# A GNN layer with a mixture of experts on one core: 18 of 49 result tiles gathered inside the edge loop

## The chip, the core and the metric

The kernel runs on one core of a Trainium2 chip. A core has a matrix engine (PE, with PEld for its weight loads), a vector engine (DVE), a scalar engine (ACT), GpSimd (POOL) and a sync engine (SP). Each takes its instructions in the order in which the program issued them. SP, ACT and POOL also issue DMAs, and a DMA that has to wait for a buffer or for another engine's result holds up everything behind it in the same queue. Times are device microseconds of one launch; lower is better.

## The reference

There are 6250 nodes with 256 features in float32 and 100000 edges, sorted by their target node. The layer is a graph step followed by a feed-forward step with experts:

```
xh  = layernorm(x)
agg = segment_sum(xh[src], dst) / max(degree, 1)
x1  = x + concat(xh, agg) @ W.T + b
xn  = layernorm(layernorm(x1)) * gamma + beta
logits = xn @ Wr + br;  two best of 8 experts, softmax over those two
out = x1 + sum over the two experts of  w_e * (gelu(xn @ W1[e] + b1[e]) @ W2[e] + b2[e])
```

Each expert has 512 hidden units. Every node thus needs its own row x1 and two rows of expert results, which lie at places that only the routing knows.

## The kernel before

**Tiles.** The 100000 edges are padded to 784 edge tiles of 128 edges: 56 windows (`W`) of 14 tiles (`C`). A window of edges belongs to at most 128 neighbouring nodes. Four windows form a chunk (14 chunks, `K`); chunks form three batches of 8, 5 and 1 chunks. For the output, the nodes are cut once more into 49 node tiles of 128 rows (the last has 106).

**Start.** The kernel multiplies all node rows by the neighbour half of W and writes the product to the DRAM tensor `z_d`; the own half goes to `u_d` a little later, in tasks that run beside the first edge tiles.

**Edge loop.** Tile `t` is handled as follows. POOL has earlier issued an indirect DMA (`gather`, line 601) that fetches 128 rows of `z_d` into buffer `xg[t % XG]`; there are `XG` = 28 such buffers, and the loop issues the gather of tile t + XG right behind the matmul of tile t, because that matmul frees the buffer. PE multiplies the buffer by a one-hot matrix that DVE built (`hot_tiles`, line 612) and adds it to the window's sum in PSUM (`add_edges`, line 618). One-hots are built half a window at a time, about half a window ahead. When a window is complete, DVE divides by the degree and adds u (`window_x1`, lines 658 to 660), and SP writes the new node rows to `x1_d` (line 661), at a row that is only known at run time. When a chunk is complete, routing follows: norms, logits, ranks, counts, one-hot matrices for sorting tokens by expert (lines 697 and 705), and a plan that is written to DRAM and read back by node tile (`plans`).

**Order by hand.** The order on all engines is written out. `at(t, f)` puts a step behind edge tile t. `after(t)` runs those steps, then expert tasks at a given pace (each task has a cost in us, and a tile allows 0.72, 0.6 in the last 56 tiles, more behind the loop), then `sum_rows`. The expert tasks of a chunk (`expert_stages`: 8 experts in pairs, lines 884, 889, 897, 901, 903) start 60 tiles behind the chunk's end, fewer for the last chunks. A batch also has a few tiles of overflow rows (`more_stages`, lines 927 to 952), which come behind its last chunk. Expert results go to the DRAM tensor `y_d`.

**The sums.** `start_experts` appends the chunk's node tiles to the list `sums`. For a node tile, `gather_rows` has SP load the 128 rows of x1 (line 973) and POOL gather two sets of 128 rows from `y_d` (line 976), into three buffers that `spare()` hands out from the ring of `xg` buffers. `add_rows` has DVE do two multiply-adds (line 983) and SP write the output (line 985). `sum_rows` issues them: it waits until the batch of the node tile has issued all its results (`batch.left` is 0) and until fewer than XG edge tiles are left, as the ring then has buffers that no edge tile needs any more:

```
while sums and not sums[0][0].batch.left and clock >= due and left < XG:
    if 0 < left < XG and spares + 3 > XG - left:
        return
```

The adds are kept in a list `adds`. One is issued when more than XG // 3 - 1 (8) node tiles wait in it or, behind the loop, when the planner's clock has come to `added`, which advances by 2.5 per node tile. Node tiles 0 to 26 belong to batch 0, 27 to 44 to batch 1, 45 to 48 to batch 2.

A branch at the end (lines 1171 to 1261) computes the same without these assumptions on the order of edges; it isn't taken here.

Of the kernel before, what the change touches and what calls it, by code (L numbers as in the profile page):

```python
# [8 lines left out]
F32 = mybir.dt.float32  # L9
# [8 lines left out]
P = 128  # L18
EPS = 1e-5
C = 14  # L20
# [4 lines left out]
BATCHES = (8, 8), (5, 5), (1, 2)  # L25
GB = 3
LATE = 40
XG = 28
RAW = 1
LATE_CHUNKS = 4  # L30

# [2 lines left out]
def gnn_ffn_kernel(ctx: ExitStack, tc: tile.TileContext, x, x_cols, src, dst, dst_next, gw, gw_t, gb, gb_cols, gamma, beta,  # L34
# [36 lines left out]
    N, D = x.shape  # L71
# [5 lines left out]
    W = src.shape[1]  # L77
# [49 lines left out]
    edges = fast_pools.enter_context(tc.tile_pool(name="edges", bufs=1))  # L127
# [6 lines left out]
    early = early_pools.enter_context(tc.tile_pool(name="early", bufs=2, side="right"))  # L134
# [31 lines left out]
    dst_i = const.tile([P, W, C], I32, name="dst_i")  # L166
    xg = [edges.tile([P, DA], F32, name=f"xg{i}") for i in range(XG)]

# [431 lines left out]
    def gather(g, c):  # L600
        nc.gpsimd.indirect_dma_start(  # L601
            out=xg[(g * C + c) % XG][:, :DZ], out_offset=None, in_=z_d[:, :],
            in_offset=bass.IndirectOffsetOnAxis(ap=src_i[:, g, c:c + 1], axis=0))
# [11 lines left out]
    def add_edges(V, c):  # L615
        if c == 0:
            V.pS = ps.tile([P, DA], F32, name="pS")
        nc.tensor.matmul(V.pS, V.hot[c // HC][:, c % HC, :], xg[(V.g * C + c) % XG],  # L618
                         start=(c == 0), stop=(c == C - 1))
# [342 lines left out]
    def spare():  # L962

        nonlocal spares
        spares += 1
        return xg[(W * C + spares - 1) % XG][:, :D]


    def gather_rows(K, n, V):
        V.rows = slice(n * P, min((n + 1) * P, N))  # L970
        count = V.rows.stop - V.rows.start
        V.o = spare()[:count]
        nc.sync.dma_start(V.o, x1_d[V.rows, :])
        V.y2 = [spare()[:count] for _ in range(2)]
        for r in range(2):
            nc.gpsimd.indirect_dma_start(  # L976
                out=V.y2[r], out_offset=None, in_=y_d[:K.batch.end_row, :],
                in_offset=bass.IndirectOffsetOnAxis(ap=plans[:count, n, r:r + 1], axis=0))

    def add_rows(n, V):  # L980
        count = V.rows.stop - V.rows.start
        for r in range(2):
            nc.vector.scalar_tensor_tensor(V.o, V.y2[r], plans.bitcast(F32)[:count, n, 2 + r:3 + r], V.o,  # L983
                                           op0=ALU.mult, op1=ALU.add)
        nc.sync.dma_start(out[V.rows, :], V.o)
# [3 lines left out]

    tasks, later, Ks, sums, adds = [], {}, [], [], []  # L990
    slots, w1_sb, w2_sb, xe = None, None, None, None
    now, spent, clock, due, added, spares = None, 0.0, 0.0, 0.0, 0.0, 0
    class Steps:

        x1, var, roots, norms, route, exps, weigh, choices, count = 2, 5, 7, 9, 11, 14, 15, 16, 19
# [15 lines left out]
    def at(t, f, *args):  # L1011
        later.setdefault(max(t, now), []).append(lambda: f(*args))
# [51 lines left out]
    def sum_rows():  # L1064

        nonlocal due, added
        if now < W * C:
            added = clock + 3.0
        while adds and now >= W * C and (added <= clock or not (sums or tasks)):
            adds.pop(0)()  # L1070
            added += 2.5
        left = W * C - 1 - now
        while sums and not sums[0][0].batch.left and clock >= due and left < XG:
            if 0 < left < XG and spares + 3 > XG - left:
                return
            K, n = sums.pop(0)
            V = Group()
            gather_rows(K, n, V)
            adds.append(lambda n=n, V=V: add_rows(n, V))
            while len(adds) > XG // 3 - 1:  # L1080
                adds.pop(0)()
                added += 2.5
            due = max(due, clock - 6.0) + (4.0 if left > 0 else 2.4)

    def after(t):
        nonlocal now, spent, clock
        now = t
        while later.get(t):
            later[t].pop(0)()
        later.pop(t, None)  # L1090
        clock += 0.6 if t < W * C else 0.3 if tasks else 1.2

        pace = 0.6 if W * C - 56 <= t < W * C else 0.72 if t < W * C else 1.2 if len(Ks) < W // CW else 2.0
        spent = min(spent + pace, pace) if tasks else 0.0
        while tasks and spent > 0:
            us, f, _ = tasks.pop(0)
            spent -= us
            clock += us
            f()
        sum_rows()  # L1100

    def new_window(g, V_before):
        V = Group()
        V.g, V.before, V.hot = g, V_before, []
        hot_tiles(V, 0)
        return V

    now = 0
    V = new_window(0, None)
# [6 lines left out]
    for index in range(W // CW):  # L1116
        K = Group()
# [9 lines left out]
        for g in range(K.first, K.first + CW):  # L1127
            if g > 0:
                V = V_next
# [41 lines left out]
    with tc.If(wrong_r > 0), tc.tile_pool(name="gp", bufs=1) as gp:  # L1171
# [9 lines left out]
        with tc.For_i(0, W * C) as j:  # L1181
# [18 lines left out]

            spare = gp.tile([P, 1], F32, name="spare")
            nc.vector.scalar_tensor_tensor(spare, lane, float(N), own, op0=ALU.add, op1=ALU.subtract)
            nc.vector.scalar_tensor_tensor(spare, count, 0.0, spare, op0=ALU.is_gt, op1=ALU.mult)
            to = gp.tile([P, 1], I32, name="to")
# [107 lines left out]
```

## Time and profile before

| what | value |
|---|---|
| time, median of 17 runs | 1197.09 us (1192.41 to 1202.67) |
| profiled execution: time | 1196.68 us |
| profiled execution: span | 1194.9 us, mean granted clock of PE 0.949 |
| PE busy | 1058.1 us (89%) |
| POOL busy | 845.4 us (71%) |
| DVE busy | 688.1 us (58%) |
| ACT busy | 463.3 us (39%) |
| software DMA queue (POOL's gathers) | 118.91 MB, 40.3% of 16 engines' span |
| first and last edge gather on POOL | 75.5 and 1046.0 us |
| first and last gather of expert rows on POOL | 1047.2 and 1182.5 us |

How to read the profile's rows: a group is "line engine operation output<-input xcount | busy us, mean ns of one | idle us of that engine just before, and what ended it". A row of the timeline is "start us, duration us, engine, line, operation, count, and in brackets the idle time before it and its releaser". A row of waits is "who <- for whom: total us, times, longest us". "issue" as releaser means that nothing in the profile was waited for. A row of a table by stretch is "from:to, length, busy us (count) for each engine, granted clock, DMA share, GB/s".

### The profile page before, as it was taken

The numbers are of one execution on the slowest core, as the hardware profiler recorded it, in microseconds if no ns is written. First come the engines' busy times: TensorE is split into PE (matmuls) and PEld (weight loads), VectorE is DVE, ScalarE is ACT, GpSimd is POOL, SyncE is SP. The second block draws the span as 40 slices with busy tenths as digits, with TensorE's granted clock in tenths as the row PEclk, the third lists the DMA queues.
The fourth block names the chain that finished last, engine by engine and source line by source line (L and its number), as shares of the span: only waits on it lengthen the run. The fifth ranks groups of instructions, "written<-read, shape, count | busy, mean of one in ns | idle before, by whom it ended". The sixth has DMA issues, their size and how long they took to land. (4 is left out here: it accounts for less than half of the span.)

```text
span 1194.9 us, 18881 instructions
## 1 busy us (share of the span) xinstructions
PE 1058.1 (89%) x5352; PEld 860.8 (72%) x5352; DVE 688.1 (58%) x2433; ACT 463.3 (39%) x1281; POOL 845.4 (71%) x892
## 2 busy tenths in 40 slices
PE   7939977899989999898999979899999999988970
PEld 6828755688858778586877858578888887875750
DVE  5757878565735555364655536465572745557642
ACT  2430001635334534443453444434552543642510
POOL 0077677777777777777777777777777777777574
PEclk9969997999989999898998989999999999997995
DMA  9978989656564564656465465554656564676784
GB/s 330 357 236 267 318 283 314 128 141 146 144 145 132 147 142 136 133 143 140 136 148 142 136 132 143 135 148 137 141 138 154 144 155 131 139 225 194 202 244 131
DMA packets 143578, 210.08 MB, mean 176 GB/s; under 512 B 36652, under 2 KB 111128, under 8 KB 143340
## 3 DMA queue, kind: packets, MB, share of 16 engines
q0 software_dynamic: 42768, 118.91, 40.3%
q1 hardware_dynamic: 92364, 80.45, 21.2%
q10 hardware_dynamic: 8336, 9.45, 2.4%
q8 instruction: 45, 0.74, 0.3%
q14 instruction: 65, 0.53, 0.1%
HBM read 163.86 MB, written 44.86 MB: 175 GB/s over the span
## 5 line engine op out<-in xcount | busy, mean ns | idle before, releaser
L601 POOL DMA_INDIRECT xg<-z_d,src_i x770 | 732.8, 952 | 237.7 <-issue 105.4
L618 PE MATMUL pS<-xg,hot 128*128 128x265 f32 x1568 | 436.1, 402 | 52.9 <-DMA xg<-z_d,src_i 28.8
L618 PEld LDWEIGHTS pS<-xg,hot 128*128 128x128 f32 x1568 | 287.0, 194 | 134.0 <-DMA xg<-z_d,src_i 49.0
L884 PEld LDWEIGHTS ph<-xe,w_sb 128*128 128x128 f32 x1792 | 224.9, 199 | 15.1 <-ACT xe L859 6.2
L884 PE MATMUL ph<-xe,w_sb 128*128 128x128 f32 x1792 | 227.4, 283 | 4.8 <-ACT xe L859 4.8
L897 PE MATMUL py<-w_sb,hid 128*128 128x256 f32 x896 | 216.4, 386 | 1.8 <-DVE rows L901 1.8
L612 DVE TENSOR_TENSOR hot<-cols,rel 128x896 f32<-128x896 f32 x112 | 121.6, 1087 | 136.6 <-PE pS L618 134.1
L889 ACT ACTIVATE hid<-ph,b_sb 128x128 f32<-128x128 f32 x448 | 127.5, 368 | 179.3 <-PE ph L884 179.0
L897 PEld LDWEIGHTS py<-w_sb,hid 128*128 128x128 f32 x896 | 170.3, 192 | 33.8 <-issue 6.8
L859 ACT ACTIVATE xe<-xs x448 | 139.3, 311 | 86.2 <-ACT xe L859 36.4
L976 POOL DMA_INDIRECT xg<-y_d,plans x98 | 96.9, 989 | 40.2 <-issue 16.2
L708 ACT ACTIVATE xs<-pm,beta_sb,gamma_sb 128x256 f32<-128x256 f32 x112 | 57.1, 560 | 133.4 <-PE pm L705 133.0
L901 DVE TENSOR_TENSOR rows<-py,b_sb 128x512 f32<-128x512 f32 x56 | 38.5, 687 | 116.2 <-PE py L897 116.1
L640 ACT ACTIVATE sums<-pS 128x265 f32<-128x265 f32 x55 | 21.3, 388 | 111.2 <-PE pS L618 108.0
L271 PE MATMUL ph<-gc,x_t 128*128 128x264 f32 (+1 forms) x200 | 57.9, 415 | 7.2 <-ACT zt L295 5.7
L705 PE MATMUL pm<-to,xn 128*128 128x256 f32 x224 | 59.0, 387 | 5.3 <-DVE to L698 5.3
L660 DVE SCALAR_TENSOR_TENSOR x<-pS,rdeg,x 128x264 f32<-128x264 f32 x55 | 27.1, 493 | 61.5 <-DMA x<-u_d 60.1
L983 DVE SCALAR_TENSOR_TENSOR xg<-xg,plans,xg 128x256 f32<-128x256 f32 (+1 forms) x98 | 45.8, 483 | 19.8 <-DMA xg<-y_d,plans 14.0
L330 POOL DMA_INDIRECT xg<-x_dram,src_i x14 | 13.4, 959 | 59.9 <-DMA src_i<-src_dram 56.0
L889 ACT ACT_TABLE_LOAD x25 | 32.1, 1283 | 55.8 <-PE ph L884 55.6
L271 PE MATMUL pm<-gc,x_t 128*128 128x264 f32 (+1 forms) x192 | 53.4, 402 | 0.0
L705 PEld LDWEIGHTS pm<-to,xn 128*128 128x128 f32 x224 | 43.2, 194 | 14.1 <-issue 4.7
(214 smaller groups left out, 889.9 us busy)
## 6 DMA issues: line engine op xcount, KB each, us to landing
y_d<-rows SPq DMA_DIRECT2D x56, 256.0 KB
xg<-z_d,src_i POOLq DMA_INDIRECT x770
w_sb<-w_dram ACTq DMA_DIRECT2D x16, 512.0 KB
x<-u_d SPq DMA_DIRECT2D x55, 132.0 KB
x_d<-x SPq DMA_DIRECT2D x55, 128.0 KB
u_d<-u_t SPq DMA_DIRECT2D x24, 264.0 KB
x_t<-x_cols_dram SPq DMA_DIRECT2D x12, 512.0 KB
xu<-x_dram SPq DMA_DIRECT2D x24, 256.0 KB
```

Of the source, the lines that this page charges most:

```text
L271: nc.tensor.matmul(pz, x_t[:, t, k, :], gc[:, h * KD + k, :n], start=(k == 0), stop=(k == KD - 1))
L601: nc.gpsimd.indirect_dma_start(out=xg[(g * C + c) % XG][:, :DZ], out_offset=None, in_=z_d[:, :], in_offset=bass.IndirectOffsetOnAxis(ap=sr ...
L612: nc.vector.tensor_tensor(hot, col[:, None, :].to_broadcast([P, HC, P]), V.rel[:, c:c + HC, None].to_broadcast([P, HC, P]), op=ALU.is_equal)
L618: nc.tensor.matmul(V.pS, V.hot[c // HC][:, c % HC, :], xg[(V.g * C + c) % XG], start=(c == 0), stop=(c == C - 1))
L705: nc.tensor.matmul(px[:, k, :], G.xn[i][:, k * P:(k + 1) * P], G.one_hot[i], start=True, stop=True)
L708: nc.scalar.activation(xs[:, at:at + 2 * P], px[:, k, :], AF.Identity, bias=beta_sb[:, k:k + 1], scale=gamma_sb[:, k:k + 1])
L859: nc.scalar.activation(xe[:, :, bass.ds(to_at, CAP)], src[:, :, bass.ds(src_at, CAP)], AF.Copy)
L884: nc.tensor.matmul(ph[:, i, a * SH:(a + 1) * SH], w1_sb[:, U.e + a, k, c * P:(c + 1) * P], xe[:, k, at:at + SH], start=(k == 0), stop=(k = ...
L889: nc.scalar.activation(U.hid[:, c, a * SH:(a + 1) * SH], ph[:, i, a * SH:(a + 1) * SH], AF.Gelu, bias=b1_sb[:, U.e + a, c:c + 1])
L897: nc.tensor.matmul(U.py[:, h, :], U.hid[:, c, h * P:(h + 1) * P], w2_sb[:, U.e + h, c, :], start=(c == 0), stop=(c == KH - 1))
L976: nc.gpsimd.indirect_dma_start(out=V.y2[r], out_offset=None, in_=y_d[:K.batch.end_row, :], in_offset=bass.IndirectOffsetOnAxis(ap=plans[:c ...
L983: nc.vector.scalar_tensor_tensor(V.o, V.y2[r], plans.bitcast(F32)[:count, n, 2 + r:3 + r], V.o, op0=ALU.mult, op1=ALU.add)
```

## The change

The number of edge buffers goes from 28 to 23, and six new buffers `yb` of 128 x 256 are added. From the moment batch 0 has issued its last result, and while more than 32 edge tiles are left, a node tile is gathered every 9 edge tiles, up to 18 of them. Such an early node tile uses three of the six `yb` buffers in turn, and its adds and its output write stand 8 edge tiles behind its gathers in the order. The other 31 node tiles are issued as before, when fewer than `XG` edge tiles (now 23) are left; their ring consists of the 23 edge buffers and the six new ones. The condition on `spares` in the last tiles of the loop, which keeps them off buffers that an edge tile still needs, now counts with 23.

```diff
-XG = 28
+XG = 23
+YB = 6
+EARLY, APART = 18, 9
...
-        return xg[(W * C + spares - 1) % XG][:, :D]
-    def gather_rows(K, n, V):
+        i = (spares - 1) % (XG + YB)
+        return xg[(W * C + i) % XG][:, :D] if i < XG else yb[i - XG]
+
+    yb = [edges.tile([P, D], F32, name=f"yb{i}") for i in range(YB)]
+
+    def early_sum():
+        nonlocal early, next_early
+        K, n = sums.pop(0)
+        V = Group()
+        kept = [yb[(3 * early + i) % YB] for i in range(3)]
+        gather_rows(K, n, V, lambda: kept.pop(0))
+        at(now + APART - 1, add_rows, n, V)
+        early += 1
+        next_early = now + APART
+
+    def gather_rows(K, n, V, spare):
...
         left = W * C - 1 - now
+        if sums and not sums[0][0].batch.left and early < EARLY and now >= next_early and left > XG + APART:
+            early_sum()
         while sums and not sums[0][0].batch.left and clock >= due and left < XG:
...
-            gather_rows(K, n, V)
+            gather_rows(K, n, V, spare)
             adds.append(lambda n=n, V=V: add_rows(n, V))
-            while len(adds) > XG // 3 - 1:
+            while len(adds) > (XG + YB) // 3 - 1:
```

With 29 buffers in the ring, the limit on node tiles waiting in `adds` stays at 8.

More of the change, by code (lines that the diff above doesn't have):

```diff
@@ L991, in gnn_ffn_kernel @@
     slots, w1_sb, w2_sb, xe = None, None, None, None
-    now, spent, clock, due, added, spares = None, 0.0, 0.0, 0.0, 0.0, 0
+    now, spent, clock, due, added, spares, early, next_early = None, 0.0, 0.0, 0.0, 0.0, 0, 0, 0
     class Steps:
```

## The prediction

> **What bounds the kernel now.** I read the page's groups first, then the waits of POOL, then the counts of edge matmuls and edge gathers side by side by stretches, and last the end of the trace queue by queue. From the page's groups:
> ```profile
> L601 POOL DMA_INDIRECT xg<-z_d,src_i x770 | 732.8, 952 | 237.7 <-issue 105.4
> L618 PE MATMUL pS<-xg,hot 128*128 128x265 f32 x1568 | 436.1, 402 | 52.9 <-DMA xg<-z_d,src_i 28.8
> L976 POOL DMA_INDIRECT xg<-y_d,plans x98 | 96.9, 989 | 40.2 <-issue 16.2
> L983 DVE SCALAR_TENSOR_TENSOR xg<-xg,plans,xg 128x256 f32<-128x256 f32 (+1 forms) x98 | 45.8, 483 | 19.8 <-DMA xg<-y_d,plans 14.0
> ```
> POOL looks 71% busy, with 238 us of idle time around its edge gathers. The timeline shows what that idle time is: in the loop and in the tail alike, one gather takes 0.95 us and the next begins 0.30 us later, whatever is named as releaser.
> ```profile
> 1043.47 0.95 POOL L601 DMA_INDIRECT xg<-z_d,src_i  x1 [0.30 <-PE pS L618]
> 1044.72 0.95 POOL L601 DMA_INDIRECT xg<-z_d,src_i  x1 [0.30 <-issue]
> 1045.97 0.95 POOL L601 DMA_INDIRECT xg<-z_d,src_i  x1 [0.30 <-PE pS L618]
> 1047.22 0.94 POOL L976 DMA_INDIRECT xg<-y_d,plans  x1 [0.30 <-PE pS L618]
> 1048.47 0.95 POOL L976 DMA_INDIRECT xg<-y_d,plans  x1 [0.30 <-issue]
> ```
> A gather therefore holds POOL for 1.25 us, and from about 160 us to 1098 us POOL has no free slot: POOL is full, not 71% full. Whether PE needs its pace is read from counts. The edge matmuls (two records each) in four stretches, with the columns PE busy (count), PEld busy (count), clock, DMA share, GB/s:
> ```profile
> 100.00:150.00 50.00, 18.61 (x68) 12.59 (x68) 1.00 0.95 301
> 300.00:350.00 50.00, 22.98 (x84) 14.79 (x83) 1.00 0.57 142
> 700.00:750.00 50.00, 20.77 (x70) 13.18 (x71) 0.93 0.51 136
> 850.00:900.00 50.00, 20.43 (x76) 13.22 (x74) 1.00 0.57 141
> ```
> Half the running sum of these counts is the tile PE has reached; POOL's is 14 plus its gathers. POOL's lead comes out as 24 tiles at 100 us, 27 at 150, 12 at 250, 3 to 6 from 300 to 700, then 7, 10, 13, 13, 11 at 750, 800, 900, 950, 1000. So there are three stages: up to about 200 us PE is behind and the 28 buffers are all filled; from 280 to 750 PE lives from hand to mouth on POOL (a gather needs 4 to 6 us to land, which is what a lead of 4 means); from 750 PE and POOL run at nearly one pace. PE's waits between 350 and 450 us (total, times, longest) say the same:
> ```profile
> PE pS L618 <- DMA xg<-z_d,src_i: 7.2, 7, 1.9
> PEld pS L618 <- DMA xg<-z_d,src_i: 10.5, 8, 2.3
> ```
> The tail: POOL's last edge gather ends at 1046.9, PE's last edge matmul about 1059.8. Batch 1's last result is copied by DVE at 1121.29. From POOL's and SP's timelines:
> ```profile
> 1114.32 0.95 POOL L976 DMA_INDIRECT xg<-y_d,plans  x1 [0.30 <-issue]
> 1120.46 0.94 POOL L976 DMA_INDIRECT xg<-y_d,plans  x1 [5.20 <-DMA out_dram<-xg]
> ...
> 1126.65 0.94 POOL L976 DMA_INDIRECT xg<-y_d,plans  x1 [0.97 <-DVE xg L983]
> ...
> 1182.54 1.56 POOL L976 DMA_INDIRECT xg<-y_d,plans  x1 [0.30 <-issue]
> ```
> From 1126.65 to 1182.54 there are exactly 44 gathers: nodes 27 to 48, all of batches 1 and 2. They cannot start before batch 1 is done (1121.29 plus 5.3 us), and none of them is moved by this change. The 18 moved nodes are gathered before, in POOL time that lies beside PE's last routing and expert work.
>
> **The change part by part.** The sum is made against the profiled run: span 1194.9, time 1196.68, 0.4 below the median of 17.
>
> 1. When the early sums run. Batch 0 is chunks 0 to 7. I stepped through the planner's own costs (0.72 per tile, 2.0, 1.75, 1.7, 0.5 per task): its last result is issued at tile 590 of 784, so the early sums stand at tiles 590, 599, ... 743, all ahead of POOL's last edge gather. PE passes tile 590 near 814 us. The same stepping gives, for the kernel before, the order of loads, output writes and y_d writes that SP's timeline shows from 1121 us on.
>
> 2. Edge loop, POOL: 36 gathers x 1.25 us = +45.0 us ahead of the last edge gather. Cover: PE's own work. Between 800 and 1050 us PE passed 199 tiles in 250 us, 1.256 us a tile; POOL would now need 1.25 + 2.5/9 = 1.53. The lead of 10 to 13 is worth some 8 tiles, 10 us, before the landing time is reached; I keep none of it, because of the next point but one. Both ends: +34 to +45.
>
> 3. 23 buffers: until about 158 us PE takes 1.37 us a tile and POOL runs into the limit; a lead of 27 becomes 22 or 23, so POOL leaves that stage 5 gathers later. From 280 us POOL is the bound and nothing gives it back: 5 x 1.25 = +6.25 us. Ends: 0 (PE late anyway) to 6.25. Ten DVE memsets fewer at the start are under 2 us of DVE beside PE's first work: nothing.
>
> 4. The wait that is added. POOL's instruction for tile t + 23 stands at program position t, so with a lead of 4 POOL is 19 positions behind PE. The two adds stand on DVE eight tiles after the gathers, and SP's output write behind them. DVE stops there until POOL has come up to that position and the rows have landed. Queued behind it are the one-hot tiles for the next window and the routing of the last chunk; PE can run on for some 3 to 13 tiles of one-hots. This costs no POOL time as long as the lead stays under 23, but it holds PE at a lead of 10 to 16 rather than 4, so the lead of point 2 isn't there to be spent. PE before ended 12.9 us after POOL's last gather; at a lead of 10 to 14 and 1.22 us a tile it is 12 to 17. I take +1.5; ends -6 and +12 (the lead reaches 23 in some windows). SP's stop at the same place delays the u loads behind it (DVE waits 60.1 us for those already, 7.6 at most); in the same ends.
>
> Loop: 45.0 + 6.25 + 1.5 = +52.75.
>
> 5. From the loop's end to batch 1's last result, 61.5 us before. DVE did 18 to 19 nodes' adds there (0.97 us each), now 9 (nodes 18 to 26). PE's idle time there is some 11 us, part of it behind DVE (at 1092 to 1097 two adds stand ahead of a one-hot and PE waits 3.63 us). I take -3; ends 0 and -9.
>
> 6. The tail from batch 1's last result, F. Before, the queue held eight nodes between gather and add: at F the planner issued gather 27 and add 19. With 18 nodes gone early, the nine late ones of batch 0 are all added before F, and at F the queue is empty. The planner's due time for adds is then long past, so each node is added at once: gathers 27, 28, 29, adds 27, 28, 29, gather 30, add 30, gather 31, and so on to 44. SP takes its queue in order, and a node's x1 load now stands behind the previous node's output write, which waits for that node's adds. One turn of this ring is two adds 0.97, the write's issue 0.4, the load's issue 0.4 and its landing, 2.2 us or more. The nearest rows for a landing are SP's own waits:
> ```profile
> SPq L661 <- DMA xg<-x_d: 5.9, 3, 2.3
> SPq L973 <- DMA x_d<-u_last: 2.7, 1, 2.7
> ```
> That makes 4.0 us a node (ends 2.5, POOL's own pace, and 5). Gathers 27 to 29 begin at F + 5.3, the sixth at F + 11.6, landing 5.2 us later (4.1 to 6.0 in the chain's rows), add 29 ends at F + 17.7. Of nodes 30 to 44 two go together, so 14 turns and one add: F + 74.7. The results of chunk 13 are copied by DVE between these adds, with one PSUM buffer, so PE's last experts go at the ring's pace. The last result is copied at about F + 77 (F + 39.7 before); first gather of nodes 45 to 48 5.3 us later, six gathers to F + 88.6, landing and adds F + 95, node 48's load behind them and its adds F + 99.3, write and end 5.8: F + 105. Before it was F + 73.6. So +31.5. If the ring does not bind, POOL begins its 44 gathers at F + 5.3 as before and saves the four gathers and the stall that stood ahead of them: 0 to -4.
>
> Sum: 52.75 - 3 + 31.5 = +81 us: span 1276, time 1278, 6.8% above.
>
> **A rule against the sum.** The row is 1.25 us of POOL for every gather. The Trainium skill, "DMA: Bandwidth & Descriptors", section on the anatomy of one DMA on the GpSimd path, puts nearly all of a transfer's fixed 2 us into the write receipt and calls descriptor generation small, with many descriptors emitted before its cost shows. By that rule the 36 gathers would hold POOL for almost nothing, part 2 would be near 0 and the sum about +36. The trace does not agree: POOL's rows stand 1.25 us apart with nothing waited for.
>
> **The rivals.**
> - A, the loop pays and the ring does not bind: +52.75 - 3 - 4 = +46, time 1243. For it: POOL's 2.5 us a node is certain, the ring is derived from the order and no stretch of the trace shows it. Against: SP's waits for "DVE xg L983" are already 36 us with eight nodes between.
> - B, the loop pays more: DVE and SP stops push the lead to 23, POOL stops too, and a ring turn is 5 us: +12 and +14 on top, time 1303. For it: PE's run-ahead is only 3 or 4 tiles where routing is due. Against: per nine tiles POOL needs 13.75 us and PE 11.4.
> - C, faster: PE sets the loop after 800 us and the 36 gathers vanish beside it, so F stays, and the tail is at most four gathers and a stall shorter, about 7.5 us: time 1189. For it: PE is 98 to 100% busy from 800 to 1000 us. It decides if the loop can swallow 45 us where the lead holds 10; POOL's 0.30 us gaps would have to be free time.
> - D, no change: POOL issues the same 868 gathers in any order, so what the loop gains the tail loses. It would need the last 44 gathers not to wait for PE; the 5.20 us stall and the 0.97 us one ahead of them speak against it. Time 1195 to 1197.
>
> **How the numbers follow.** The forecast 0.54, A 0.28, B 0.12, C 0.04, D 0.02. The forecast's own range is 1260 to 1296 (turns of 3.5 to 4.8 us, loop +46 to +58). A's 1243 with -5 for the lead is 1238; B cut at its lower half gives 1302. A measurement of this kernel can tell about 0.2%, 2.4 us, from no change; faster 0.04, same 0.01, slower 0.95.
>
> **What would show it.** POOL at one gather per 1.25 us through the loop, its last edge gather near 1098 us; PE waiting for "DMA xg<-z_d" past 800 us too; DVE adds with waits for "DMA xg<-y_d" between 820 and 1060 us; lead 10 or more there; batch 1's last copy near 1171; after it SP alternating load and output write every 4 us and DVE adds waiting for "DMA xg<-x_d"; and the last copy of batch 2 some 77 us after F. Wrong would be: POOL gaps that shrink below 0.30 us, a first gather of node 27 near 1127, or adds after F at 2.5 us a node.

## The result and the profile after

The changed kernel takes 1280.1 us (median of 8 runs, 1277.5 to 1283.8); the kernel before takes 1197.1 us (median of 46). The ratio is 1.0697, with a 95% interval of 1.0679 to 1.0715. The forecast was 1278. The profiled run after has a span of 1275.8 us against 1194.9 before, so 80.9 us have to be found.

The page's groups after. The lines have moved by two in the loop (L601 is now L603, L618 is L620) and by more further down: L990 gathers expert rows, L997 is the two adds, L899 and L903 are an expert's second matmul and the copy of its result.

```profile
L603 POOL DMA_INDIRECT xg<-z_d,src_i x770 | 733.6, 953 | 243.1 <-issue 110.3
L620 PE MATMUL pS<-xg,hot 128*128 128x265 f32 x1568 | 444.0, 408 | 72.8 <-DMA xg<-z_d,src_i 36.7
L899 PE MATMUL py<-w_sb,hid 128*128 128x256 f32 x896 | 230.1, 404 | 39.5 <-DVE rows L903 36.1
L990 POOL DMA_INDIRECT yb<-y_d,plans x48 | 45.6, 950 | 99.7 <-DMA yb<-x_d 55.3
```

A gather still holds POOL for 0.95 us. New are 36 us in which PE waited for DVE's copies of expert results, and 100 us in which POOL stood idle ahead of gathers of expert rows into `yb`, 86 of them in two waits. POOL's timeline has them:

```profile
1098.60 0.94 POOL L603 DMA_INDIRECT xg<-z_d,src_i  x1 [0.30 <-issue]
1099.85 0.94 POOL L990 DMA_INDIRECT xg<-y_d,plans  x1 [0.30 <-issue]
...
1121.33 0.94 POOL L990 DMA_INDIRECT yb<-y_d,plans  x1 [0.30 <-DVE newton L190]
1177.61 0.94 POOL L990 DMA_INDIRECT yb<-y_d,plans  x1 [55.34 <-DMA yb<-x_d]
...
1221.78 0.95 POOL L990 DMA_INDIRECT xg<-y_d,plans  x1 [0.30 <-issue]
1253.03 0.94 POOL L990 DMA_INDIRECT yb<-y_d,plans  x1 [30.31 <-DMA y_d<-rows]
...
1262.41 1.56 POOL L990 DMA_INDIRECT xg<-y_d,plans  x1 [0.30 <-issue]
```

The last edge gather starts at 1098.6 us (1046.0 before). After the 18 gathers for the last node tiles of batch 0 POOL has nothing to do until batch 1 is done. Then 36 gathers run at POOL's pace, and it waits 30 us more for batch 2. So the POOL time that the early gathers freed in the tail is spent idle.

Where the loop's time went is seen when POOL's start of the gather for one and the same edge tile is taken from both timelines (us):

```
tile     14    64   114   264   414   564   614   664   714   764   783
before  75.5 141.4 206.3 395.3 583.3 771.1 833.8 896.7 959.5 1022.2 1046.0
after   76.6 149.6 213.7 402.8 590.8 778.3 843.5 919.4 997.0 1072.3 1098.6
later    1.1   8.2   7.4   7.5   7.5   7.2   9.7  22.7  37.5   50.1   52.6
```

Two steps are there and little else: 7.4 us lost by tile 114, and never given back; then 45.2 us over the tiles beside which the 36 early gathers stand, 1.256 us for each. Of the 7.4 us, 1.1 are there at the first gather; the rest is lost while POOL runs into the limit of its buffers and waits for PE's edge matmuls to free one. POOL's waits between 70 and 165 us (total, times, longest), before and after:

```profile
POOL xg L601 <- PE pS L618: 10.1, 23, 1.5
POOL xg L603 <- PE pS L620: 16.5, 26, 1.5
```

In the stretch of the early gathers, from 820 to 1100 us, no gap between POOL's instructions is longer than 0.3 us: POOL doesn't wait there, it is full.

In that stretch PE does not wait for gathers. Its longest waits there, with total, times and longest:

```profile
PE pS L620 <- DVE hot L614: 14.9, 3, 7.7
PE pm L680 <- DVE both L674: 12.4, 2, 8.9
PE py L899 <- DVE rows L903: 6.7, 4, 3.1
```

All of PE's waits for DVE come to 38.5 us there; on the same edge tiles in the kernel before (810 to 1045 us) they come to 3.1. And over the whole run DVE, which carries the adds, waits for the expert rows, 96.4 of the 109.8 us at the early adds:

```profile
DVE yb L997 <- DMA yb<-y_d,plans: 109.8, 36, 10.6
DVE xg L997 <- DMA xg<-x_d: 39.9, 13, 5.9
```

POOL's shortage thus reaches PE through DVE, which stands at the early adds until POOL has come up to their gathers. PE's distance behind POOL, from the counts of both in the stretches from 0, doesn't show this: it is 3 tiles at 700 us in both kernels, and with the early adds 8, 15, 9, 14 and 7 at 850, 900, 950, 1000 and 1050; but the kernel before, where PE itself is 98 to 100% busy from 800 to 1000 us, has 11, 14, 13.5, 12 and 8.5 at these times.

The second of these rows, the waits for x1 (`x_d`), is the tail. SP's and DVE's timelines, behind batch 1's last copy at 1174.55 us:

```profile
1192.09 0.33 SPq L999 DMA_DIRECT2D out_dram<-xg  x1
1192.52 0.39 SPq L987 DMA_DIRECT2D xg<-x_d  x1
1196.09 0.33 SPq L999 DMA_DIRECT2D out_dram<-xg  x1
1196.51 0.38 SPq L987 DMA_DIRECT2D xg<-x_d  x1
1200.17 0.33 SPq L999 DMA_DIRECT2D out_dram<-xg  x1
```
```profile
1191.06 1.00 DVE L997 SCALAR_TENSOR_TENSOR xg<-xg,plans,xg 128x256 f32<-128x256 f32 x2 [3.78 <-DMA xg<-x_d]
1195.06 1.00 DVE L997 SCALAR_TENSOR_TENSOR xg<-xg,plans,xg 128x256 f32<-128x256 f32 x2 [2.99 <-DMA xg<-x_d]
1199.12 1.02 DVE L997 SCALAR_TENSOR_TENSOR xg<-xg,plans,xg 128x256 f32<-128x256 f32 x2 [3.06 <-DMA xg<-x_d]
```

Two adds, the output write, the next node tile's load of x1, its landing, two adds: a ring, with a turn about every 4 us. From 1191.06 to 1245.86 there are 13 turns, 4.2 us each. PE's expert work of the last chunk goes at that pace, since its results are copied by DVE between the adds:

```profile
1184.95 3.73 PE L886 MATMUL ph<-xe,w_sb 128*128 128x128 f32 x32
1205.51 5.23 PE L899 MATMUL py<-w_sb,hid 128*128 128x256 f32 x16 [16.82 <-DVE rows L903]
```

The last copy of batch 2 comes 75.4 us after that of batch 1 (39.7 before), the end 101.3 us after it (73.6 before).

### The profile page after: what moved, and what is told of

Same layout as the page of the kernel before. It is cut to its first block, busy times and chain, and to the rows that moved or that the text cites. A ratio compares the mean times of both kernels' runs of the same rounds, so it can differ in the third digit from the quotient of the medians.

```text
span 1275.8 us, 18854 instructions
## 1 busy us (share of the span) xinstructions
PE 1076.0 (84%) x5352; PEld 867.6 (68%) x5352; DVE 689.4 (54%) x2423; ACT 463.1 (36%) x1281; POOL 844.0 (66%) x892
## 5 line engine op out<-in xcount | busy, mean ns | idle before, releaser
L603 POOL DMA_INDIRECT xg<-z_d,src_i x770 | 733.6, 953 | 243.1 <-issue 110.3
L620 PE MATMUL pS<-xg,hot 128*128 128x265 f32 x1568 | 444.0, 408 | 72.8 <-DMA xg<-z_d,src_i 36.7
L620 PEld LDWEIGHTS pS<-xg,hot 128*128 128x128 f32 x1568 | 290.4, 197 | 159.3 <-DMA xg<-z_d,src_i 56.7
L899 PE MATMUL py<-w_sb,hid 128*128 128x256 f32 x896 | 230.1, 404 | 39.5 <-DVE rows L903 36.1
L899 PEld LDWEIGHTS py<-w_sb,hid 128*128 128x128 f32 x896 | 179.0, 203 | 77.2 <-DVE rows L903 25.8
L886 PEld LDWEIGHTS ph<-xe,w_sb 128*128 128x128 f32 x1792 | 220.6, 196 | 12.4 <-ACT xe L861 3.8
L886 PE MATMUL ph<-xe,w_sb 128*128 128x128 f32 x1792 | 223.2, 279 | 2.6 <-ACT xe L861 2.6
L614 DVE TENSOR_TENSOR hot<-cols,rel 128x896 f32<-128x896 f32 x112 | 121.5, 1087 | 104.5 <-PE pS L620 101.3
L990 POOL DMA_INDIRECT yb<-y_d,plans x48 | 45.6, 950 | 99.7 <-DMA yb<-x_d 55.3
L903 DVE TENSOR_TENSOR rows<-py,b_sb 128x512 f32<-128x512 f32 x56 | 38.4, 685 | 92.2 <-PE py L899 92.2
L997 DVE SCALAR_TENSOR_TENSOR yb<-yb,plans,yb 128x256 f32<-128x256 f32 x45 | 21.8, 485 | 113.0 <-DMA yb<-y_d,plans 109.8
L662 DVE SCALAR_TENSOR_TENSOR x<-pS,rdeg,x 128x264 f32<-128x264 f32 x55 | 27.1, 493 | 60.4 <-DMA x<-u_d 59.0
L990 POOL DMA_INDIRECT xg<-y_d,plans x50 | 49.2, 983 | 15.2 <-issue 11.0
L273 PEld LDWEIGHTS ph<-gc,x_t 128*128 128x128 f32 x200 | 39.3, 201 | 20.3 <-ACT zt L297 9.1
```

Source lines behind the costliest of these rows:

```text
L273: nc.tensor.matmul(pz, x_t[:, t, k, :], gc[:, h * KD + k, :n], start=(k == 0), stop=(k == KD - 1))
L603: nc.gpsimd.indirect_dma_start(out=xg[(g * C + c) % XG][:, :DZ], out_offset=None, in_=z_d[:, :], in_offset=bass.IndirectOffsetOnAxis(ap=sr ...
L614: nc.vector.tensor_tensor(hot, col[:, None, :].to_broadcast([P, HC, P]), V.rel[:, c:c + HC, None].to_broadcast([P, HC, P]), op=ALU.is_equal)
L886: nc.tensor.matmul(ph[:, i, a * SH:(a + 1) * SH], w1_sb[:, U.e + a, k, c * P:(c + 1) * P], xe[:, k, at:at + SH], start=(k == 0), stop=(k = ...
L899: nc.tensor.matmul(U.py[:, h, :], U.hid[:, c, h * P:(h + 1) * P], w2_sb[:, U.e + h, c, :], start=(c == 0), stop=(c == KH - 1))
L903: nc.vector.tensor_tensor(ys, U.py, b2_sb[:, U.e:U.e + 2, :], op=ALU.add)
```

## The experiments

In none of the experiments did the kernel before come near the 1197 us of the runs above ("the first runs" below). It takes 1411 to 1431 us, on three chips, numbered 5, 7 and 8 here; which chip the first runs had is not known. The difference is not the chip alone: on chip 5 the same kernel took 1411.1 us in one set of runs and 1430.6 in the next. In the profiled run on chip 7, PE's waits without a releaser come to 122 us (none in the first runs), with matmuls that stand 1.4 us apart, and PE is busy for 1126.8 us instead of 1058.1, at a granted clock of 0.893 instead of 0.949. So each run is held against the runs of the kernel before beside it. Profiles of the kernel before and the changed kernel are from chip 7 alone, so a difference in profile to a run on chip 5 or 8 also holds the difference between sets. The table has, from each run's profile: the end of the last edge gather on POOL, the end of PE's last edge matmul, the last copy of batch 1 (F), the time from F to the span's end, and the two medians.

| kernel (chip) | last edge gather | PE's last edge matmul | F | F to end | median | before beside it |
|---|---|---|---|---|---|---|
| the kernel before (7) | 1232.4 | 1261.9 | 1329.8 | 90.7 | 1419.3 | 1412.1 |
| the changed kernel (7) | 1278.2 | 1300.3 | 1359.9 | 113.0 | 1478.4 | 1412.1 |
| 9 early node tiles (7) | 1252.2 | 1275.6 | 1338.1 | 96.9 | 1442.1 | 1412.1 |
| adds kept back (5) | 1277.2 | 1300.0 | 1353.6 | 91.5 | 1449.0 | 1411.1 |
| adds kept back, again (5) | 1293.3 | 1316.0 | 1369.6 | 94.4 | 1466.6 | 1430.6 |
| early gathers alone (5) | 1274.1 | 1296.5 | 1360.6 | 91.5 | 1456.9 | 1411.1 |
| early gathers alone, again (5) | 1287.6 | 1309.1 | 1373.6 | 93.2 | 1468.9 | 1430.6 |
| no early gathers, but adds (5) | 1228.9 | 1251.3 | 1310.8 | 114.3 | 1427.9 | 1411.1 |
| early adds later (5) | 1282.2 | 1305.1 | 1366.6 | 115.2 | 1477.3 | 1411.1 |
| no early node tiles (5) | 1235.9 | 1259.3 | 1325.1 | 90.9 | 1417.3 | 1430.6 |
| before, adds at once (8) | 1242.9 | 1272.4 | 1342.3 | 125.1 | 1463.4 | 1426.7 |
| before, batches of 9, 4, 1 (5) | 1234.0 | 1260.2 | 1344.7 | 90.2 | 1444.0 | 1430.6 |

**The kernel before and the changed kernel there.** 

> The kernel before unchanged, for its profile on the chip on which it takes 1411 to 1431 us. Theory: PE's own pauses, not POOL, set the edge loop there (POOL's gathers wait for PE at places after 300 us), tail from batch 1's last copy to the end 88 to 95 us. Rival: POOL has no free slot there either, the gathers themselves are slower.

> The changed kernel unchanged, run beside the others on the chip on which the kernel before takes 1411 to 1431 us, as an anchor for them. Theory (loop and tail are separate terms that hold there too): the +36 to +38 of the kernel with late adds plus 23 to 37 for the ring, +60 to +75 us, last copy of batch 1 to the end near 115 us. Rival (the terms overlap where PE pauses): +36 to +50.

The changed kernel costs 66.2 us more there, a ratio of 1.0486 (1.0449 to 1.0524), inside the +60 to +75; the tail is 113.0 us. The same source as the kernel before came out at 1.0060 (1.0038 to 1.0083) beside it, so two copies of one program differ by 7 us within one set, and differences of that size mean nothing here. What limits the loop is not what it was in the first runs: POOL's lead in the kernel before is 24.5, 25, 24.5 and 27 tiles at 700, 900, 1000 and 1100 us, so POOL stands near its limit of 28 and waits for PE (138.5 us in all for edge matmuls, 68.6 in the first runs), as the theory of that expectation had it.

**The adds behind the loop kept back.** The popping by the planner's clock is replaced by the queue of eight of the kernel before:

```diff
-        while adds and now >= W * C and (added <= clock or not (sums or tasks)):
+        while adds and now >= W * C and (len(adds) > 8 or not (sums or tasks)):
```

> The changed kernel with the adds behind the loop kept eight node tiles behind their gathers, as they were before; edge loop untouched. Theory (loop +54, then a ring of output write, load and add at 4.2 us a node): the ring goes, the tail from batch 1's last copy to the end falls from 101 to some 71 to 74 us, time 1250 (1247 to 1254). Rival (PE's last experts or POOL set the tail, the adds only follow): 1280, no change.

> The changed kernel with the adds behind the loop kept eight node tiles behind their gathers, as they were before; edge loop untouched. It ran once on a chip on which PE paused without a cause in the profile and the kernel before took 1411 us; wanted is a run against a kernel before near 1197. Theory: the ring goes, the tail from batch 1's last copy to the end falls from 101 to some 71 to 74 us, 1250 (1247 to 1254), a ratio of 1.042 to 1.047. Rival (PE's last experts or POOL set the tail): 1280, a ratio of 1.07.

The second run met a kernel before at 1430.6 us, not the wanted 1197. The two ratios are 1.0272 (1.0226 to 1.0318) and 1.0274 (1.0224 to 1.0324), against 1.0486 of the changed kernel: the order of the adds alone is worth some 29 us. The tail falls from 113.0 to 91.5 and 94.4 us, near the 90.7 of the kernel before; another 6 us are saved ahead of it, from PE's last edge matmul to F (53.6 us in both runs, 59.6 in the changed kernel). In the first of the two the edge loop ends where the changed kernel's does, to 0.3 us. SP no longer stands between a write and the next load:

```profile
1384.20 0.34 SPq L987 DMA_DIRECT2D xg<-x_d  x1
1384.63 0.40 SPq L999 DMA_DIRECT2D out_dram<-yb  x1
1385.13 0.38 SPq L987 DMA_DIRECT2D yb<-x_d  x1
1385.60 0.60 SPq L999 DMA_DIRECT2D out_dram<-xg  x1
```

The time saved is as expected, 29 us for 30; of the tail only 19 to 22 us went, for 27 to 30. The ratios lie below the 1.042 to 1.047 that was written for a kernel before near 1197, as the loop costs less here; that range was not tested.

**The ring put into the kernel before.** Nothing is moved into the loop; once batch 1 is done, adds follow their gathers at once:

```diff
-            while len(adds) > XG // 3 - 1:
+            while len(adds) > (XG // 3 - 1 if K.batch is batches[0] else 0):
```

> The kernel before, nothing moved into the edge loop; the only edit is that once batch 1 is done a node tile's adds and output write are issued right behind its gathers instead of eight node tiles later, which is what the change brings about by emptying that queue. Theory (the ring of output write, load and adds is what costs in the tail): the tail from batch 1's last copy to the end grows from 73.6 to about 100 us, 1223 to 1229 where the kernel before takes 1197, +22 to +30 us where it takes 1411 to 1431. Rival (the tail's loss comes with the moved gathers, not with the order of adds): within 5 us of the kernel before.

1463.4 against 1426.7 us, +36.8 us, a ratio of 1.0250 (1.0228 to 1.0273): a little more than expected, and far from the rival. The tail is 125.1 us, 34 more than in the kernel before on chip 7. SP's timeline has the ring, and DVE the wait:

```profile
1404.43 0.34 SPq L985 DMA_DIRECT2D out_dram<-xg  x1
1404.86 0.38 SPq L973 DMA_DIRECT2D xg<-x_d  x1
1408.06 0.34 SPq L985 DMA_DIRECT2D out_dram<-xg  x1
1408.49 0.38 SPq L973 DMA_DIRECT2D xg<-x_d  x1
1411.69 0.34 SPq L985 DMA_DIRECT2D out_dram<-xg  x1
```
```profile
DVE xg L983 <- DMA xg<-x_d: 45.9, 14, 5.8
```

3.6 us a turn where no copy of an expert result lies between. With the run before, this shows the tail's price from both sides: taken out of the changed kernel it goes, put into the kernel before it comes, and the moved gathers are not needed for it.

**The early gathers alone, and all but the early gathers.** In the first kernel an early step issues its two gathers into unused buffers and nothing else, and all 49 node tiles are summed at the end; in the second the early step keeps its load, adds and write, and the two gathers are left out, so that 18 node tiles get no expert rows:

```diff
-        K, n = sums.pop(0)
...
-        gather_rows(K, n, V, lambda: kept.pop(0))
-        at(now + APART - 1, add_rows, n, V)
+        K, n = sums[early]
+        for r in range(2):
+            nc.gpsimd.indirect_dma_start(
+                out=yb[(2 * early + r) % YB], out_offset=None, in_=y_d[:K.batch.end_row, :],
+                in_offset=bass.IndirectOffsetOnAxis(ap=plans[:, n, r:r + 1], axis=0))
```
```diff
-        gather_rows(K, n, V, lambda: kept.pop(0))
+        gather_rows(K, n, V, lambda: kept.pop(0), False)
...
-        for r in range(2):
+        for r in range(2 if fetch else 0):
```

> The changed kernel, but the early node tiles get only their 36 gathers (two of the six buffers in turn, results unused): no x1 load, no adds, no output write in the loop, and all 49 node tiles are summed at the end as before. Theory (a gather holds POOL 1.25 us): last edge gather near 1099 us as in the changed kernel, PE closer behind it than 14.6 us because DVE and SP do not stop, tail as before the change (73 us from batch 1's last copy): 1243 to 1250. Rival (what costs in the loop is DVE and SP stopping for the early sums, gathers ride along): 1197 to 1205.

> The changed kernel with the 36 early gathers alone: no early x1 load, adds or output write, and all 49 node tiles summed at the end as before. Theory (a gather holds POOL 1.25 us): last edge gather near 1099 us, tail of 73 us from batch 1's last copy: 1243 to 1250, a ratio of 1.038 to 1.044. Rival (DVE and SP stops are the loop's cost): 1197 to 1205.

> The changed kernel with the early node tiles' 36 gathers left out, their loads, adds and output writes kept at their places (the two expert rows of these 18 node tiles are not fetched, the adds take stale buffers). Theory: the loop loses its 45 us, the ring in the tail stays at +28: 1228 to 1236. Rival (DVE and SP stops are the loop's cost): 1265 to 1280. Rival (ring and loop are coupled, the tail's 28 us come with the loop): 1200 to 1210.

The gathers alone cost 45.8 and 38.3 us (ratios 1.0333, 1.0295 to 1.0370, and 1.0292, 1.0246 to 1.0338) and leave the tail at 91.5 and 93.2 us; the adds without gathers cost 16.8 us (1.0119, 1.0083 to 1.0155) and have the long tail, 114.3 us. Both prices are at the foot of the expected ones or below them (46 to 53 us, and 31 to 39 us, on a kernel before at 1197); the 16.8 us alone would lie nearer to the rival in which ring and loop are coupled, and it is the tail, 24 us longer than the 90.7 of the kernel before with no gather in the loop, that speaks against it. Between the two, which ran together, the last edge gather differs by 45.2 us, the size of 36 gathers at 1.256 us. So the loop's price belongs to the gathers and the tail's to the order of the adds, and each comes without the other; the rivals that put the loop's price on the stops of DVE and SP, or coupled the two, fall. One thing doesn't fit. Here POOL stood near its limit (its lead was 20 and 18 of 23 tiles at 900 us, with and without the gathers), so the theory's reason, a POOL without a free slot, does not hold here, and the gathers should have been partly hidden. From 960 us to the last edge gather PE's unexplained pauses ahead of one expert matmul grew instead from 8.1 to 27.1 us, its busy time from 237.9 to 256.2 us, and its granted clock fell from 0.95 to 0.90. Why PE pays for gathers here stays open. That POOL's time is the reason in the first runs is not shown by an experiment; it rests on the table of starts above and on POOL's gaps, none of which is longer than 0.3 us there.

**The early adds later.**

```diff
-        at(now + APART - 1, add_rows, n, V)
+        at(now + 2 * APART - 1, add_rows, n, V)
```

> The changed kernel with the early adds and output writes 17 instead of 8 edge tiles behind their gathers, just before the buffers are used again. POOL stands some 19 tiles behind PE in the order when it is the bound, so DVE and SP then hardly stop. Theory: POOL's pace is the same, its last edge gather stays near 1099 us, PE follows it by 8 to 13 us instead of 14.6: 1274 to 1280. Rival (the stops cost POOL time, as the lead reaches 23): last edge gather earlier by several us and 1260 to 1272.

1.0465 (1.0429 to 1.0500) against the changed kernel's 1.0486: no difference that can be told. Neither sign came: the rival needs an earlier last edge gather (it is at 1282.2, against 1278.2 us in the changed kernel), the theory a PE that follows it more closely (22.9 against 22.1 us). This does not decide what the stop of DVE costs, as there was little of it here: up to the end of its loop DVE waits 2.4 us in 2 times for rows in `yb` in the changed kernel on chip 7, where in the first runs it was 96.4 us in 31.

**No early node tiles, 23 buffers.**

```diff
-EARLY, APART = 18, 9
+EARLY, APART = 0, 9
```

> The changed kernel with the number of early node tiles set to 0: 23 edge buffers and six spare ones, all sums at the end. By step 3 of the prediction as written (POOL leaves the first stage 5 gathers later and nothing gives it back): 1203. Rival (the lead of 10 to 13 tiles that PE has behind 800 us swallows it, and buffers only cost together with the early gathers): 1196 to 1199.

0.9914 (0.9890 to 0.9938), 13 us less than the kernel before, which neither side had expected. It is about twice the 7 us by which two copies of one program differ, so half of it may be scatter; what the rest is was not found. Against the profile of the kernel before on chip 7 the loop's end is 2.6 us earlier and the tail the same. The buffers' price was not measured by it.

**Nine early node tiles.**

```diff
-EARLY, APART = 18, 9
+EARLY, APART = 9, 9
```

> The changed kernel with 9 instead of 18 early node tiles. By the planner's order three node tiles then still stand between gather and add when batch 1 is done, so the ring doesn't close. Theory: half of the loop's price and none of the tail's: +18 to +27 us over the kernel before, 0 to 5 us more in the tail. Rival (the price goes with the number of early node tiles alone): half of what the changed kernel costs beside it, +30 to +37.

1.0217 (1.0197 to 1.0237), +30.0 us, but +22.9 against the identical kernel beside it: the time decides for neither. The profile is clearer: the last edge gather is 19.8 us later than in the kernel before, less than half of the changed kernel's 45.8, and the tail 6.2 us longer, where the changed kernel's is 22.3. With three node tiles between gather and add the ring is mostly open, as the theory had it.

**A version with more node tiles ready early.** Since the gathers that wait for batch 1 fill the tail of the first runs, batch 0 was made one chunk larger in the kernel before:

```diff
-BATCHES = (8, 8), (5, 5), (1, 2)
+BATCHES = (9, 9), (4, 4), (1, 2)
```

> The kernel before with chunks in batches of 9, 4 and 1 instead of 8, 5 and 1, overflow tiles moved with them (9, 4, 2). Nodes 27 to 30 then belong to batch 0 and are gathered in the POOL time between the last edge gather and batch 1's last result, in which POOL stood still for 10 us; 36 gathers instead of 44 remain behind that result, and batch 1 has one overflow tile less. Theory (what matters is how many gathers wait for batch 1): 5 to 10 us less, 1187 to 1192. Rival (the last batch's result sets the end, or POOL's time before is taken anyway): 1195 to 1199.

1.0132 (1.0084 to 1.0180): no gain, and 13 us more, again about twice what two copies of one program differ by. 36 gathers stand behind F instead of 44, as planned, but the tail is 90.2 us, with 90.7 in the kernel before on chip 7, because here batch 2's last copy comes only 64.5 us after F (64.7 in that run) and sets the end; F itself is 15 us later than there, but the kernel before takes 11 to 18 us longer in this set too. What it would do where that distance is 39.7 us is open. No version was faster than the kernel before by more than the 19.5 us by which the kernel before itself differs between two sets on chip 5.

## Why the prediction was right

The sum had five terms; their sizes in the profiled first runs:

| term | predicted | measured |
|---|---|---|
| 36 gathers on POOL in the loop | +45.0 | +45.2 |
| 23 buffers | +6.25 | +7.4 |
| PE's distance behind POOL at the loop's end | +1.5 | +1.7 (14.8 against 13.1) |
| loop's end to batch 1's last copy | -3 | -1.1 (60.2 against 61.3) |
| tail behind it | +31.5 | +27.6 |
| sum | +81 | +80.9 (before rounding) |

That the sums agree to 0.1 us is luck: the tail was taken 3.9 us too long, and points 3 and 5 together 3 us too short. That each term has its sign and nearly its size is not.

- **POOL is full.** The first reading, that 0.30 us between gathers is no free time, carried the forecast. 36 gathers of 1.25 us were paid in full. Rival C, which needed the loop to swallow them, is out, and so is D, in which the tail gains what the loop loses. The Trainium skill ("DMA: Bandwidth & Descriptors", anatomy of one DMA) calls descriptor generation "small, variable". Read as in the prediction, that would make these gathers almost free; the trace decides against that reading: each cost 1.256 us, of which POOL's instruction is 0.95.
- **The buffers (point 3).** POOL left the first stage 7.4 us later and kept that to tile 564, as the point had it; 1.1 us of it was there at the first edge gather, and the rest, 6.3, is the 6.25 of the point. That PE would not make it good later holds only because the early gathers made POOL the bound again; the kernel with 23 buffers alone was to test it and could not.
- **The wait that is added (point 4).** DVE did stop at the early adds, for 96 us in all, and PE waited 38.5 us for DVE beside them (3.1 before). Two of the signs that I gave were wrong: PE was to wait for "DMA xg<-z_d" past 800 us too, and waited for DVE's one-hots, routing and copies instead; and a lead of 10 or more is no sign, since the kernel before has 8.5 to 14 tiles there as well. The stop takes the place of the wait for gathers. That the time is POOL's either way is argued from POOL's gaps; no run took the stop away where POOL is full.
- **Loop's end to F (point 5)** was mis-sized by 2 us. Nine node tiles' adds fewer did not shorten PE's waits for DVE by much: PE still waited 4.46 us for "DVE both" and 2.55 us for "DVE to" there (3.63 and 3.63 before).
- **The tail (point 6)** had the mechanism and was 4 us too long. The first gathers came 3.1 us behind F, not 5.3; the adds of nodes 27 to 29 stood 2.8 to 3.3 us behind the start of their gathers, not the 5.2 that I took from the chain's rows. In the trace before, adds that waited for their rows came 2.8 to 3.2 us behind the gather for nodes 44 to 47, and 5.1 to 6.1 for nodes 35, 41, 42 and 48; why they differ is not shown. So the adds of node 29 ended at F + 12.7 and not F + 17.7. The ring was a little slower, 4.2 us a turn for 4.0. Batch 2's last copy came at F + 75.4 for the predicted 77. Rival A, in which the ring doesn't bind, is what the kernel with the adds kept back is, some 29 us faster than the changed one. Rival B has turns of 5 us and a lead of 23 tiles; neither came.

## What to carry to other kernels

An engine that shows 71% busy can be full: look at the gap between its instructions where nothing is waited for, and count work in slots of instruction plus gap. Work moved from a tail into a loop saves tail time only if the tail's work was waiting for that engine and not for a late result; here 44 gathers waited for batch 1, and none of them was moved. And when a queue of deferred work runs empty, a pipeline of depth eight becomes a chain of depth one, though no line of the code that is waited in has changed.

## What the runs showed that I had not expected

- One program takes 1197 us in the first runs and 1411 to 1431 us in all later ones, on three chips. In the later ones PE issues matmuls one at a time, 1.4 us apart, in stretches of up to 18 us, with no releaser in the profile (columns as in the timelines above, from the kernel with the adds kept back):

```profile
1376.61 0.37 PE L886 MATMUL ph<-xe,w_sb 128*128 128x128 f32 x1 [0.85 <-issue]
1378.01 0.37 PE L886 MATMUL ph<-xe,w_sb 128*128 128x128 f32 x1 [1.03 <-issue]
1379.41 0.37 PE L886 MATMUL ph<-xe,w_sb 128*128 128x128 f32 x1 [1.03 <-issue]
1380.81 0.37 PE L886 MATMUL ph<-xe,w_sb 128*128 128x128 f32 x1 [1.03 <-issue]
```

- In those runs 36 gathers cost 45.2 us of loop although POOL was waiting for PE; longer pauses and a lower clock of PE came with them. No run shows the connection, or whether the slower runs go with the chip.
